# A planned attention kernel: other slots for weight sums, residual loads and one normalisation, and other issuers for six transfers

## The chip, the cores and the metric

The kernel runs on one core of a Trainium2 chip. The metric is the device time of one execution in microseconds (us). A core has five engines with queues of their own: PE (TensorE, matrix products into the accumulator memory PSUM), DVE (VectorE), ACT (ScalarE), POOL (GpSimd) and SP (SyncE, which only issues transfers here). Transfers (DMAs) are issued by SP or by POOL and run beside the engines. An engine works through its own queue in order.

## The reference

For 8 batches of 256 rows with 1024 features, a cross attention with 32 heads of 32 features. Keys and values are the same context tensor:

```
xn  = (x - mean) * rsqrt(var + eps) * gamma + beta
Q   = xn @ Wq.T                 # 32 heads
P   = softmax(mask(Q K^T / sqrt(32)))
out = x + (P V) @ Wout.T
```

All of it is float32.

## The kernel before

**Blocks and slots.** The work is cut into 64 blocks of four heads, n = 0 to 63; batch b owns blocks 8b to 8b+7. The main loop has one slot per block. In slot n PE runs `scores(n + 1)` (16 products, tiles `sc`), some steps of the output projection of an earlier batch (`po_A`, `po_S`), `values(n - 2)` (64 products, tiles `pv`), and products that make queries of a later batch (`pq`, `pq_A`, `pq_S`). In the times below a slot begins with the first score product of block n+1. The scores of a block fill all four PSUM tiles `sc`, so scores of block n+1 can enter a tile only after DVE has taken block n's scores from it.

**Softmax of a block** (`softmax_parts`). For each of four heads j, DVE adds the mask and takes the minimum (L634, `e<-sc,mb`), ACT takes the exponential and its sum (L638), DVE takes the reciprocal (L648, `rden`), and POOL scales the two halves (L654, `e<-e,rden`), or ACT does where the plan's list `scaled` names the pair (block, j) (L652). DVE transposes the result in 32x32 blocks (L660, `pT<-e`), ACT copies half of it aside (L666, `pc<-pT`), and transfers swap the halves between partitions: first `pT<-pT` ("A"), then `pT<-pc` ("B"), both issued at L740. ACT also copies finished queries (`qa`) and values (`at`).

**What else runs beside it.** Batches 1 and 2 are normalised and transposed beside the blocks of batch 0. `ln_stats` takes the statistics on DVE (L339 to L344) and `rstd` on POOL (L347). `ln_norm` applies them, on DVE or POOL in one instruction (L365), or on ACT (L360) after a small instruction on POOL (L357, `shift`). `fold` multiplies a column of Wq by gamma on POOL (L474, 128x1024). From batch 3 on, queries and all output projections use a seven-product scheme in which sums of weight blocks replace an eighth product. `sum_wo` (L290) and `sum_wq` (L504) make these sums, 128x512 each, on the engine that the plan names: P is POOL, V is DVE, A is ACT.

**What sets the order.** A table `PLAN` gives every piece a slot. Inside a slot each engine's order is that of the program text. Entries are relative to the slot in which a batch's query products begin (18 for batch 3, then 26, 34, 42, 50). `wq` and `wo` hold [slot, sum, column, engine]; `foldat` the slot of each fold; `b2`, `b3` and `rel` the slots of loads, statistics, normalisations and transposes of a batch; `st0` and `stg` how many of the 28 projection steps of a batch stand in each of three places of nine slots; `rs0` and `rs` the slots in which four residual tiles `r` are loaded, relative to the batch's first projection slot; `p1late` the batches whose first residual tile is finished later. `keeps` sends finished sums to DRAM.

**Who issues a transfer.** The table `qp`, read in `issue` (L211, L213) and in `swap` (L740, L645), names exceptions to SP: 1 is POOL at once, 2 is POOL at the end of the slot (the call at L1268), and 3 for a swap is POOL just before the next block's first POOL scaling. The swap in question is `sB04`: block 4, first half, back. In a block's tail the order on SP is: swaps A, the loads of the list `between` (keys, rings, residuals, x, weights), swaps B. Residual tiles rotate through four buffers, so a load into one waits until the result that lay there has been sent out; a wait on SP holds everything behind it, swaps B among them. A key load or a residual tile is 256 KB, a value load 512 KB, the two transfers of a swap 128 KB each.

```python
rp = ctx.enter_context(tc.tile_pool(name="rp", bufs=...4))
...
for r in range(2):
    swap(r, False)
for load in between:
    load()
for r in range(2):
    swap(r, True)
```

Of the kernel before, what the change touches and what calls it, by code (L numbers as in the profile page):

```python
# [33 lines left out]


# [1 line left out]
PLAN = {'wq': [[9, 'T1', 0, 'P'], [14, 'T1', 1, 'V'], [15, 'T1', 3, 'V'], [16, 'T3', 2, 'V'], [14, 'T1', 2, 'P'],  # L37
# [13 lines left out]
 'folds': 'PPPPPPPP',  # L51
 'b2': {'loads': [0, 0],
        'stats': [2, 3],
        'norms': [2, 3],
        'trans': [4, 5],
        'moves': [5, 5, 5, 5, 5, 5, 6, 6, 6, 6, 6, 6, 7, 7, 7, 7]},
 'b3': {'loads': [-13, -11],
        'stats': [-10, -9],
        'norms': [-9, -7],
        'trans': [-7, -6],  # L60
        'moves': [-6, -6, -6, -6, -5, -5, -5, -5, -4, -4, -4, -4, -4, -4, -3, -3]},
 'norm2': 'PV',
 'norm3': 'AA',
 'SPLIT': 3,
 'rings': [[-3, -4], [0, 0], [2, 2]],
 'foldat': [-1, 1, 3, 3, 4, 5, 6, 7],
 'st0': [0, 0, 0, 0, 6, 1, 0, 1, 1, 0, 3, 3, 0, 1, 0, 0, 1, 1, 0, 2, 1, 0, 3, 0, 0, 4, 0],
 'stg': [0, 0, 0, 0, 4, 4, 0, 0, 4, 0, 0, 1, 0, 3, 0, 0, 0, 3, 0, 1, 4, 0, 0, 0, 0, 4, 0],
 'rel': {'loads': [-13, -12],
         'stats': [-11, -9],  # L70
         'norms': [-9, -8],
# [1 line left out]
         'moves': [-6, -6, -6, -6, -6, -6, -6, -5, -5, -5, -5, -4, -4, -4, -4, -4]},  # L73
 'woload': [[0, 0, 3], [3, 1, 1], [3, 0, -1], [0, 1, 1], [2, 0, 2], [2, 1, 2]],
 'n11': 'V',
 'p1late': [2, 0],
 'qp': {'sB04': 3,
        'out00': 2,
        'out01': 2,
        'out10': 2,  # L80
        'out11': 2,
# [7 lines left out]
        'r1_01': 2,  # L89
        'mv15': 1,  # L90
        'x1None': 2,
        'mv3_2': 2},
 'vearly': {'30': 'z',
            '44': 'b',
            '54': 'a',
# [5 lines left out]
            '12': 'z',  # L101
            '48': 'a',
            '2': 'z',
            '58': 'b',
            '26': 'b',
            '8': 'a',
            '28': 'z',
            '32': 'b',
            '52': 'b',
            '42': 'b',  # L110
            '38': 'z'},
 'rs': [0, 0, 0, -1],
 'rs0': [0, 1, 2, 3]}

# [15 lines left out]
P = 128  # L130
# [7 lines left out]
def xattn_kernel(  # L138
# [29 lines left out]
    xp = ctx.enter_context(tc.tile_pool(name="xp", bufs=2))  # L168
    rp = ctx.enter_context(tc.tile_pool(name="rp", bufs=PLAN.get('bufs',{}).get('rp',4)))
    lnp = ctx.enter_context(tc.tile_pool(name="lnp", bufs=2))  # L170
    kp = ctx.enter_context(tc.tile_pool(name="kp", bufs=2))
    vp = ctx.enter_context(tc.tile_pool(name="vp", bufs=PLAN.get('bufs',{}).get('vp',2)))
    atp = ctx.enter_context(tc.tile_pool(name="atp", bufs=3))
    ep = ctx.enter_context(tc.tile_pool(name="ep", bufs=PLAN.get('bufs',{}).get('ep',4)))
    ptp = ctx.enter_context(tc.tile_pool(name="ptp", bufs=PLAN.get('bufs',{}).get('ptp',3)))
    asp = ctx.enter_context(tc.tile_pool(name="asp", bufs=PLAN.get('bufs',{}).get('asp',3)))
    up = ctx.enter_context(tc.tile_pool(name="up", bufs=1))
# [23 lines left out]
    xs, ks, vs, rs = {}, {}, {}, {}  # L201
    QP = PLAN.get('qp', {})
    at_end = []
# [1173 lines left out]
```

## Time and profile before

| what | value |
|---|---|
| median of 3 runs | 579.17 us (578.04 to 580.08) |
| the profiled execution's own time | 579.36 us |
| its span, first to last instruction | 577.5 us |
| mean granted TensorE clock | 1.000 |
| instructions | 19967 |
| DVE, ACT, POOL busy | 82%, 74%, 69% of the span |
| DMA: bytes moved, mean rate | 116.93 MB, 202 GB/s |

A row of the timeline reads: start in us from the span's start, duration, engine, line of the kernel, operation, written tile <- read tiles, shape, count; in brackets the idle time of the engine before it and who ended that. A row of the windows reads: stretch, its length, and for each engine the busy time and the number of instructions, then granted clock, share of the DMA engines and GB/s. A row of the groups ends with busy time, mean duration in ns, and idle time before. 1.86 us of the execution's own time lie outside the span.

### The profile page before, as it was taken

To read this page: it belongs to the slowest core of one execution; us is meant where nothing else is said; L and a number is where in the kernel's file an instruction comes from. 1 tells how busy PE (TensorE), PEld (TensorE's weight loads), DVE (VectorE), ACT (ScalarE), POOL (GpSimd) and SP (SyncE) were. 2 spreads that over 40 slices of the span, in tenths; PEclk is the share of its full clock that TensorE was granted. 3 is DMA by queue.
4 is the path that set the end of the run, shared out by engine and by line. 5 is a ranking of instruction groups with operands and counts; after the bars stand their busy time and mean duration, and the time that the engine had idled before them with its cause. 6 is when DMAs were issued, how large, how long until landed. Compare 5 with 4: busy or idle time off the path is not lost.

```text
span 577.5 us, 19967 instructions
## 1 busy us (share of the span) xinstructions
PE 568.4 (98%) x7162; PEld 395.1 (68%) x7162; DVE 470.9 (82%) x1706; ACT 430.0 (74%) x1477; POOL 397.5 (69%) x648
## 2 busy tenths in 40 slices
PE   8999999999999999999999999999999999999997
PEld 8788775667667676678676677667776776755543
DVE  5899799988878889988889888888878687779823
ACT  4697878778588876888588877789868687769820
POOL 2668779888684894866759764596556676358780
PEclk9999999999999999999999999999999999999999
DMA  8767877557687667876698666877577757645751
GB/s 309 261 197 226 233 192 200 155 166 213 192 256 228 182 185 214 249 216 198 185 251 261 192 198 187 251 241 218 163 218 219 206 165 189 183 134 144 191 158 74
DMA packets 45667, 116.93 MB, mean 202 GB/s; under 512 B 9072, under 2 KB 9840, under 8 KB 45568
## 3 DMA queue, kind: packets, MB, share of 16 engines
q1 hardware_dynamic: 42256, 105.61, 63.4%
q0 software_dynamic: 3024, 10.03, 5.3%
q8 instruction: 57, 0.93, 0.7%
q14 instruction: 42, 0.34, 0.2%
q10 hardware_dynamic: 288, 0.01, 0.0%
HBM read 64.23 MB, written 11.53 MB: 131 GB/s over the span
## 4 chain that ended last, share of the span: by engine, by line
PE 64%; DVE 10%; POOL 8%; ACT 6%; DMA 5%; issue 4%; SPq 2%; DVEq 0%; POOLq 0%; ACTq 0%
PE po_S L868 13%; PE pq_A L555 12%; PE po_A L868 9%; PE sc L594 8%; PE pv L778 7%; POOL e L654 6%; PE pq_S L555 5%; PE pq L453 4%; DVE e L634 3%; DMA pT<-pT 3%; ACT e L638 3%; DVE pT L660 3%; PE po_end L935 2%; ACT e L652 1%; SPq L211 1%
## 5 line engine op out<-in xcount | busy, mean ns | idle before, releaser
L654 POOL TENSOR_SCALAR e<-e,rden 128x256 f32<-128x256 f32 x458 | 212.4, 481 | 133.9 <-DVE rden L648 127.2
L638 ACT ACTIVATE e<-e,mn 128x256 f32<-128x256 f32 x512 | 254.0, 501 | 50.1 <-DVE mn L634 50.0
L660 DVE STREAM_TRANSPOSE pT<-e 128x512 f32<-128x512 f32 x256 | 180.5, 707 | 55.2 <-POOL e L654 38.0
L634 DVE CUSTOM_DVE_ANT_0 e<-sc,mb 128x256 f32<-128x256 f32 x512 | 185.1, 415 | 17.8 <-PE sc L594 17.8
L666 ACT COPY pc<-pT 128x512 f32<-128x512 f32 x128 | 79.0, 617 | 56.9 <-DVE pT L660 37.6
L638 ACT ACTIVATION_READ_ACCUMULATOR e<-e,mn 128x1 f32 x512 | 97.9, 191 | 0.0
L453 PE MATMUL pq<-xnT,wq 128*128 128x256 f32 (+1 forms) x368 | 84.2, 382 | 1.7 <-POOL wq L474 0.9
L453 PEld LDWEIGHTS pq<-xnT,wq 128*128 128x128 f32 x368 | 68.7, 190 | 16.8 <-issue 5.0
L594 PE MATMUL sc<-k,qa 32*128 32x256 f32 x1024 | 76.2, 401 | 0.2
L778 PE MATMUL pv<-pT,v 64*32 64x128 f32 x4096 | 74.1, 274 | 0.4 <-PE sc L594 0.4
L868 PE MATMUL po_S<-wo,at 128*128 128x512 f32 x152 | 73.1, 607 | 0.7 <-DVE r L910 0.7
L594 PEld LDWEIGHTS sc<-k,qa 32*128 32x128 f32 x1024 | 47.6, 184 | 37.7 <-issue 16.8
L778 PEld LDWEIGHTS pv<-pT,v 64*32 64x32 f32 x4096 | 57.0, 105 | 23.4 <-issue 14.9
L868 PE MATMUL po_A<-wo,at 128*128 128x512 f32 x128 | 58.5, 602 | 0.6 <-DVE qa L571 0.4
L868 PE MATMUL po_S<-wo,s 128*128 128x512 f32 x104 | 47.9, 597 | 0.0
L555 PEld LDWEIGHTS pq_A<-xnT,wq 128*128 128x128 f32 x352 | 40.6, 192 | 4.9 <-issue 2.5
L868 PEld LDWEIGHTS po_S<-wo,at 128*128 128x128 f32 x152 | 26.3, 190 | 25.2 <-issue 23.9
L634 DVE DVE_READ_ACCUMULATOR2_ANT mn<- 128x1 f32 x512 | 42.1, 82 | 0.0
L555 PE MATMUL pq_A<-xnT,wq 128*128 128x128 f32 x352 | 41.6, 276 | 0.4 <-DVE wq L504 0.4
L868 PEld LDWEIGHTS po_A<-wo,at 128*128 128x128 f32 x128 | 23.3, 190 | 27.2 <-issue 25.1
L648 DVE RECIPROCAL rden<-den 128x2 f32<-128x2 f32 x256 | 37.3, 146 | 2.2 <-ACT e L638 1.5
L791 ACT COPY at<-pv 128x128 f32<-128x128 f32 x128 | 26.2, 253 | 8.7 <-PE pv L778 8.7
(109 smaller groups left out, 654.2 us busy)
## 6 DMA issues: line engine op xcount, KB each, us to landing
v<-in_kv_dram SPq DMA_DIRECT2D x32, 512.0 KB, 5.2
pT<-pT SPq DMA_DIRECT2D x128, 128.0 KB, 3.1
pT<-pc SPq DMA_DIRECT2D x127, 128.0 KB, 3.9
k<-in_kv_dram SPq DMA_DIRECT2D x32, 256.0 KB, 4.5
ring<-kept_T SPq DMA_DIRECT2D x15, 512.0 KB, 5.4
r<-in_x_dram SPq DMA_DIRECT2D x27, 256.0 KB, 5.4
xnT<-xe SPq DMA_DIRECT2D x89, 64.0 KB, 2.5
x<-in_x_dram SPq DMA_DIRECT2D x11, 512.0 KB, 4.6
```

Source lines behind the costliest of these rows:

```text
L453: nc.tensor.matmul(pqs[n], wq[:, o, c, :], xnTs[b](c), start=(c == 0), stop=(c == NC - 1),)
L555: nc.tensor.matmul(pqs[b][:, o, :], w[:, c], x_[:, c], start=begins and o + c == 0, stop=c == NK - 1, skip_group_check=True,)
L594: nc.tensor.matmul(scs[n][j][:, s, :], qa[r, n % NQ, ts(s, P)], ks[n - n % 2][r, n % 2, :], start=True, stop=True,)
L634: nc.vector.tensor_tensor_reduce(out=e[:, s, :], in0=pss[j][:, s, :], in1=mbs[n // NQ], scale=1.0, scalar=NO_SCORE, op0=ALU.add, op1=ALU.m ...
L638: nc.scalar.activation(e[:, s, :], e[:, s, :], AF.Exp, bias=mn[:, s : s + 1], scale=-1.0, accum_out=den[:, s : s + 1],)
L648: nc.vector.reciprocal(rden, dens[j])
L654: engine.tensor_scalar(es[j][:, s, :], es[j][:, s, :], rden[:, s : s + 1], 1.0, ALU.mult, ALU.mult,)
L660: nc.vector.transpose(pT[:, :, :, j, :, :].rearrange("p a i s k -> p (a i) s k"), es[j].rearrange("p s (b t) -> p b s t", t=K),)
L666: nc.scalar.copy(pc[:, :, ts(j, 2)], pT[:, 1, :, ts(j, 2)])
L778: nc.tensor.matmul(pvs[n][r][j * HD : (j + 1) * HD], vs[n - n % 2][ts(r, 2 * K), n % 2, i, ts(j, HD)], pT[ts(r, 2 * K), :, i, j, :, :], st ...
L791: nc.scalar.copy(ats[b, k][:, c, :, ts(r, 2), :], pv.rearrange("p a s k -> p s a k"))
L868: nc.tensor.matmul(po, operand(b, name)[:, c], wo[:, which, c], start=begins and c == 0, stop=c == NK - 1, skip_group_check=not begins,)
```

## The change

Only the table `PLAN` changes; no function does.

- `qp`: the entry for swap `sB04` goes, so SP issues this swap like all others. Three come in: the key loads of blocks 28, 36, 44 and 52 (`k%4`) and a copy of weight sums to DRAM (`keptT31`) are issued by POOL at once, the value load of block 56 by POOL at the slot's end.
- `norm2`: the second half of batch 2 is normalised by ACT instead of DVE (slot 3).
- `wq`: the sums T1 column 3 (slot 15) and T3 column 3 (slot 18) go from DVE to POOL, T4 column 3 (slot 22) from POOL to DVE. The other entries of `wq`, and all of `wo`, keep slot and engine and stand in another order in the list.
- `foldat`: the fold of column 1 goes from slot 1 to slot 0.
- `b3`: the first x load of batch 3 is planned for slot 4 instead of 5, its first normalisation for slot 10 instead of 9.
- `scaled`: one pair more, block 51, j = 1, from POOL to ACT.
- `st0`, `stg`: projection steps of batch 0 in other places of slots 9 to 15; for batches 2 to 5 one step goes from the ninth slot to the eighth, and one changes place within the second.
- `rs0`, `rs`: residual tiles in other slots. For batches 1 to 6, two tiles are loaded in the first projection slot and two in the next, instead of one in the slot before and three in the first.
- `p1late`: batch 3 instead of batch 2 finishes its first residual tile late. `vearly`: the value loads of blocks 58 and 52 stand elsewhere among the loads of their slot.

```diff
- 'wq': ... [15, 'T1', 3, 'V'] ... [18, 'T3', 3, 'V'] ... [22, 'T4', 3, 'P']
+ 'wq': ... [15, 'T1', 3, 'P'] ... [18, 'T3', 3, 'P'] ... [22, 'T4', 3, 'V']
+ 'scaled': ... [51, 1, 'A']
- 'b3': {'loads': [-13, -11], ... 'norms': [-9, -7],
+ 'b3': {'loads': [-14, -11], ... 'norms': [-8, -7],
- 'norm2': 'PV',
+ 'norm2': 'PA',
- 'foldat': [-1, 1, 3, 3, 4, 5, 6, 7],
- 'st0': [0, 0, 0, 0, 6, 1, 0, 1, 1, 0, 3, 3, 0, 1, 0, 0, 1, 1, 0, 2, 1, 0, 3, 0, 0, 4, 0],
- 'stg': [0, 0, 0, 0, 4, 4, 0, 0, 4, 0, 0, 1, 0, 3, 0, 0, 0, 3, 0, 1, 4, 0, 0, 0, 0, 4, 0],
+ 'foldat': [-1, 0, 3, 3, 4, 5, 6, 7],
+ 'st0': [0, 0, 0, 0, 6, 2, 0, 0, 1, 0, 3, 2, 0, 2, 0, 0, 0, 2, 0, 2, 2, 0, 2, 0, 0, 4, 0],
+ 'stg': [0, 0, 0, 0, 5, 3, 0, 0, 4, 0, 0, 1, 0, 3, 0, 0, 0, 3, 0, 1, 4, 0, 0, 1, 0, 3, 0],
- 'p1late': [2, 0],
- 'qp': {'sB04': 3, ...
+ 'p1late': [0, 3],
+ 'qp': {... 'k%4': 1, 'v56': 2, 'keptT31': 1},
- 'vearly': {... '58': 'b', ... '52': 'b', ...
+ 'vearly': {... '58': 'a', ... '52': 'z', ...
- 'rs': [0, 0, 0, -1],
- 'rs0': [0, 1, 2, 3]}
+ 'rs': [0, 1, 1, 0],
+ 'rs0': [0, 0, 2, 3]}
```

More of the change, by code (lines that the diff above doesn't have):

```diff
@@ L36 @@
 import math
-PLAN = {'wq': [[9, 'T1', 0, 'P'], [14, 'T1', 1, 'V'], [15, 'T1', 3, 'V'], [16, 'T3', 2, 'V'], [14, 'T1', 2, 'P'],
[2 rows of a table removed]
+PLAN = {'wq': [[9, 'T1', 0, 'P'], [14, 'T1', 1, 'V'], [15, 'T1', 3, 'P'], [14, 'T1', 2, 'P'], [16, 'T3', 2, 'V'],
[2 rows of a table added]
         [20, 'T2', 3, 'P']],
[2 rows of a table removed]
[2 rows of a table added]
         [7, 4, 0, 'P'], [12, 6, 3, 'P'], [10, 6, 0, 'P'], [13, 3, 0, 'V']],
@@ L56 @@
         'moves': [5, 5, 5, 5, 5, 5, 6, 6, 6, 6, 6, 6, 7, 7, 7, 7]},
- 'b3': {'loads': [-13, -11],
+ 'b3': {'loads': [-14, -11],
         'stats': [-10, -9],
-        'norms': [-9, -7],
+        'norms': [-8, -7],
         'trans': [-7, -6],
         'moves': [-6, -6, -6, -6, -5, -5, -5, -5, -4, -4, -4, -4, -4, -4, -3, -3]},
- 'norm2': 'PV',
+ 'norm2': 'PA',
  'norm3': 'AA',
@@ L75 @@
  'n11': 'V',
- 'p1late': [2, 0],
- 'qp': {'sB04': 3,
-        'out00': 2,
+ 'p1late': [0, 3],
+ 'qp': {'out00': 2,
         'out01': 2,
@@ L91 @@
         'x1None': 2,
-        'mv3_2': 2},
+        'mv3_2': 2,
+        'k%4': 1,
+        'v56': 2,
+        'keptT31': 1},
  'vearly': {'30': 'z',
@@ L103 @@
             '2': 'z',
-            '58': 'b',
+            '58': 'a',
             '26': 'b',
@@ L108 @@
             '32': 'b',
-            '52': 'b',
+            '52': 'z',
             '42': 'b',
             '38': 'z'},
- 'rs': [0, 0, 0, -1],
- 'rs0': [0, 1, 2, 3]}
+ 'rs': [0, 1, 1, 0],
+ 'rs0': [0, 0, 2, 3]}
 from contextlib import ExitStack
```

12 rows, old and new, of the table PLAN are left out of this document.

## The prediction

> **What bounds the kernel now.** I began with the busy table of the page, then had the timeline of PE for the start of each slot, then the windows by slot, and then the timelines of single engines where a slot is too long.
>
> ```profile
> PE 568.4 (98%) x7162; PEld 395.1 (68%) x7162; DVE 470.9 (82%) x1706; ACT 430.0 (74%) x1477; POOL 397.5 (69%) x648
> ```
>
> PE is busy nearly always, so the time is PE's work plus PE's stalls, and the stalls hide in slots that are longer than a twin with the same products. Columns of the windows: stretch, length, then busy time (instructions) of PE, PEld, DVE, ACT, POOL, clock, DMA share, GB/s.
>
> ```profile
> 50.62:58.16 7.54, 7.54 (x106) 6.09 (x105) 6.82 (x24) 3.78 (x14) 6.92 (x6) 1.00 0.61 190
> 58.16:66.07 7.91, 7.58 (x105) 6.08 (x104) 5.55 (x18) 5.74 (x21) 5.53 (x9) 1.00 0.90 242
> 66.07:74.79 8.72, 8.66 (x106) 6.64 (x105) 7.51 (x33) 8.06 (x29) 7.42 (x9) 1.00 0.67 194
> 74.79:83.33 8.54, 8.04 (x105) 6.35 (x105) 8.01 (x24) 5.66 (x21) 5.95 (x10) 1.00 0.92 226
> 83.33:92.90 9.57, 8.66 (x105) 6.44 (x104) 8.51 (x36) 8.43 (x33) 9.10 (x15) 1.00 0.81 207
> 180.91:190.51 9.60, 9.60 (x121) 6.69 (x120) 8.77 (x29) 7.80 (x26) 5.91 (x12) 1.00 0.89 283
> 207.73:216.23 8.50, 8.50 (x119) 6.24 (x118) 7.97 (x29) 5.51 (x20) 8.38 (x14) 1.00 0.61 155
> 216.23:226.36 10.13, 9.04 (x119) 6.23 (x118) 9.37 (x28) 6.24 (x23) 6.44 (x11) 1.00 0.89 241
> 243.24:253.16 9.92, 9.53 (x121) 6.75 (x120) 8.86 (x30) 8.94 (x27) 8.04 (x15) 1.00 0.72 229
> 311.71:321.08 9.37, 9.37 (x122) 6.62 (x121) 8.39 (x30) 8.43 (x27) 8.74 (x16) 1.00 0.57 171
> ```
>
> Slots 4 to 8 (first five rows) do equal work. Against slot 4's 7.54 the next four lose 0.37, 1.18, 1.00 and 2.03, together 4.58 us. Slot 23 loses 10.13 - 8.50 = 1.63 against slot 22. Slots 19 and 26 lose 0.23 and 0.55 against slot 34 (last row). So about 7 us are to be had in these slots; nearly all others run at PE's pace, and there a saving on another engine is worth nothing.
>
> **The change, part by part.**
>
> *Slots 3 to 9: the normalisation and the swap.* Two engines lose time here, DVE and POOL.
>
> ```profile
> 50.77 0.70 DVE L660 STREAM_TRANSPOSE pT<-e 128x512 f32<-128x512 f32 x1
> 52.16 2.38 DVE L365 TENSOR_SCALAR x<-x,mv,rstd 128x1024 f32<-128x1024 f32 x1 [0.69 <-POOL rstd L347]
> 54.45 0.41 DVE L634 CUSTOM_DVE_ANT_0 e<-sc,mb 128x256 f32<-128x256 f32 x1
> 61.37 0.71 DVE L660 STREAM_TRANSPOSE pT<-e 128x512 f32<-128x512 f32 x1 [2.14 <-POOL e L654]
> 63.73 0.39 DVE L634 CUSTOM_DVE_ANT_0 e<-sc,mb 128x256 f32<-128x256 f32 x1
> 51.55 0.57 POOL L347 TENSOR_TENSOR rstd<-ve,mhalf 128x1 f32<-128x1 f32 x1
> 52.09 4.20 POOL L474 TENSOR_TENSOR wq<-wq,gs 128x1024 f32<-128x1024 f32 x2
> 56.59 1.28 POOL L290 TENSOR_TENSOR wo<-wo 128x512 f32<-128x512 f32 x1 [0.31 <-DMA wo<-in_woT_dram]
> 59.60 0.74 POOL L645 DMA_DIRECT2D pT<-pc  x1 [1.73 <-DMA pT<-pT]
> 60.40 1.84 POOL L654 TENSOR_SCALAR e<-e,rden 128x256 f32<-128x256 f32 x4
> 54.97 0.51 ACT L638 ACTIVATE e<-e,mn 128x256 f32<-128x256 f32 x1 [3.76 <-DVE mn L634]
> L360 ACT ACTIVATE x<-x,shift,rstd 128x1024 f32<-128x1024 f32 x10 | 12.4, 1240 | 0.5
> 33.03 3.67 POOL L654 TENSOR_SCALAR e<-e,rden 128x256 f32<-128x256 f32 x8 [2.66 <-DVE rden L648]
> ```
>
> DVE is done with block 4 at 51.47 but waits 0.69 and then spends 2.38 on the normalisation while POOL folds, so block 5 begins at 54.45. Without it DVE can begin when the scores are there, whose slot starts at 50.62; 51.8 is my estimate. The work goes to ACT, which idles for 3.76 until 54.97: POOL's `rstd` ends at 52.12, the one-column `shift` takes no longer than `rstd` itself (0.57), ACT's part 1.24, so ACT's first exponential of block 5 starts by 53.9, at least 1.0 earlier. Cover: this idle stretch; without it the price is 1.24.
>
> That gain alone would stop at POOL. POOL's sum ends at 56.59 + 1.28 = 57.87; then it waits 1.73 for swap A, issues swap `sB04` in 0.74, and only at 60.40 scales block 5. With the swap on SP it can start at 57.87, its first sum of exponentials being ready by then: 2.53 earlier. SP takes one issue more, of about 0.5, between transfers that wait for swap A anyway. DVE's transpose at 61.37 waited for exactly this scaling; the third one then meets ACT's scaling and queue, so of 2.53 I keep 2.3 for block 6's start (63.73 to about 61.4). Ends: 0, if ACT or a transfer holds block 5 just as long, and 2.53.
>
> What is PE's share? PE waits in slot 6 for block 6's score tiles, at the end of slot 8 for a fold:
>
> ```profile
> 66.07 2.32 PE L594 MATMUL sc<-k,qa 32*128 32x256 f32 x16
> 89.25 3.72 PE L453 MATMUL pq<-xnT,wq 128*128 128x256 f32 x16 [0.86 <-POOL wq L474]
> ```
>
> With softmax 2.3 earlier, slot 6 begins at 65.7 with the tiles free; slots 5, 6 and 7 then lose about 0, 0 and 0.2 instead of 0.37, 1.18 and 1.00. Then late is softmax again: ACT is busy for 8.06 in slot 6, DVE for 8.01 in slot 7, POOL for 9.10 in slot 8, all more than PE's 7.54, so slot 8's stalls, the fold among them, move earlier but stay. PE wins **2.35** (2.55 less 0.2). The fold moved to slot 0 (4.20 / 2 = 2.1 at most) fits into the 2.66 that POOL idles ahead of block 2 (row of 33.03) and is worth 0; without that gap it would cost its own length.
>
> The Trainium skill, page "ScalarE: Activation LUTs", section "Rules for kernel authors", sends multiplies and adds to VectorE, not ScalarE, which speaks against `norm2`. By that rule the edit would cost the difference of the two engines; the row of 2.38 shows the opposite for this place. The page "SBUF — State Buffer", section "Who interferes with whom", gives a reason (DVE in a two-port mode and POOL shut each other out for a whole instruction), and the trace agrees here.
>
> *Weight sums.* DVE's sum T1 at slot 15 goes to POOL, as does T3 at slot 18; T4 at slot 22 comes to DVE.
>
> ```profile
> 156.85 0.68 DVE L504 TENSOR_TENSOR ring<-wq 128x512 f32<-128x512 f32 x1
> 160.24 1.29 PE L594 MATMUL sc<-k,qa 32*128 32x256 f32 x16
> 216.02 1.28 POOL L844 TENSOR_TENSOR at<-at 128x512 f32<-128x512 f32 x1
> 216.35 2.34 DVE L584 TENSOR_SCALAR mb<-mk 128x256 f32<-128x256 uint8 x1
> 217.25 1.28 POOL L504 TENSOR_TENSOR wq<-wq 128x512 f32<-128x512 f32 x1
> 218.61 1.28 DVE L504 TENSOR_TENSOR wq<-wq 128x512 f32<-128x512 f32 x2
> 219.94 3.84 PE L555 MATMUL pq_A<-xnT,wq 128*128 128x128 f32 x32 [0.42 <-DVE wq L504]
> 224.45 1.98 PE L868 MATMUL po_S<-wo,at 128*128 128x512 f32 x4 [0.67 <-DVE r L910]
> ```
>
> At slot 17's start PE's scores take 1.29 and slip behind DVE; 0.6 less DVE work just before them gives 0.2 to 0.35, of which I take **0.3**. Slot 19's 0.23 is a wait for DVE too, and the T3 sum just ahead goes: **0.2**. POOL's added sums (1.28 each) fill idle time before its next block. Slot 22: the mask bias on DVE is held until POOL's two sums end (217.25 + 1.28 = 218.53) and is over 0.16 later. With the second gone it is free at 217.30; then come 0.16 and three sums of 0.64: 219.4 instead of 219.9, so DVE begins block 24 between 0.4 and 0.5 earlier. PE's first stall (0.42) goes, its second (0.67) waits for a DVE addition at the end of the same chain and grows; the net is the chain's **0.4**. Were the mask bias slow for another reason, the third sum would cost 0.64.
>
> *Residual tiles, POOL's issues, steps.* On SP three residual loads in the first projection slot wait for a buffer:
>
> ```profile
> 239.59 5.68 SPq L211 DMA_DIRECT2D r<-in_x_dram  x3
> 364.22 1.15 SPq L740 DMA_DIRECT2D pT<-pc  x2
> 371.48 1.16 PE L778 MATMUL pv<-pT,v 64*32 64x128 f32 x64
> L1268 POOL DMA_DIRECT2D x<-in_x_dram x3 | 1.7, 571 | 0.0
> ```
>
> Two of them move a slot on, when the buffers are free, so swaps B come some 4 us earlier. This is worth 0 to PE: even the tightest swap (second half issued at about 364.8) leaves 6.6 us until its values run at 371.48. The four keys cost POOL 0.57 each ahead of a sum, with POOL waiting for DVE soon after; slot 26's stall comes from a value load, and the bytes around it stay about equal, so I count 0 (between +0.9, one more 256 KB ahead of it at the 283 GB/s of slot 19, and -0.55). The projection steps only change places; PE's total is the same, and the slots that get shorter follow longer ones. Pair (51, 1), `keptT31`, `v56`, x of batch 3, `p1late`: 0, all beside slots at PE's pace.
>
> Sum: 2.35 + 0.3 + 0.2 + 0.4 = 3.25. The profiled execution's own 579.36 less 3.25 is 576.1; it stands 0.19 above the median, which gives **575.9**.
>
> **The rivals.**
>
> *The lead grows.* Being ahead, softmax might not fall behind again, and slots 7 to 9 lose nothing. For: POOL then meets fewer collisions. Against: the busy times of 8.01 to 9.10 above, which no lead shortens. It adds 0.2 + 2.03: 573.7.
>
> *The lead is given back.* Block 5 is held by something not shown as a wait now, the sum's weight load (POOL already waits 0.31 for it) or ACT, to within 1 us of today. PE keeps about 1.0 of 2.35 and the other gains shrink to 0.3: 579.17 - 1.3 = 577.9, no measurable change.
>
> *Slower: transfers land too late.* POOL's key loads go out about 4 us sooner, the residuals are no longer held, and both run beside swaps. Swaps land in 3.9 (first row below); a value load in that crowd took 8.4 (second row).
>
> ```profile
> pT<-pc SPq DMA_DIRECT2D x127, 128.0 KB, 3.9
> DMA to landing us min/median/max: 8.4/8.4/8.4
> ```
>
> PE waits from a landing of 6.6 on. At 8.4 each of the four slots would lose 1.8, and with 0.9 for the late value load, 8.1 come against 3.25: 584.0. It turns the sign from 7.4 us of landing (3.25 / 4 + 6.6). Against it: the bytes are the same. The Trainium skill, page "DMA: Bandwidth & Descriptors", section "Issuing engines are not separate DMA queues", says that another issuer saves only issue time, as all share 16 DMA engines; by that rule the key loads bring no gain, and I count none.
>
> **How the numbers follow.** Forecast 0.56, lead grows 0.15, given back 0.16, slower 0.13. 0.3% is 1.7 us, about what a measurement of this kernel can tell from no change. Faster: 0.56 + 0.15 = 0.71, same 0.16, slower 0.13. The range must leave out no more than 0.2: it runs from 573.2 (lead grows, and 0.5 of slot 26) to 579.1 (given back, with 0.9 for the late value load and none of the 0.3), and leaves the slower case out. The forecast's own bounds, 2.53 and 0 on its largest term, lie inside.
>
> **What would show it.** After the change slots 5, 6 and 7 last 7.5 to 7.8, slot 8 still over 9; block 5's first exponential on ACT comes before 54 and POOL's scaling of it before 58.5; no POOL row L645; the mask bias of slot 22 below 1.5; slot 23 near 9.7; residual loads on SP without a wait of 3 us. I am wrong if slot 6 or 7 is still over 8.3, or if values (L778) begin to wait for swaps after slot 24.

## The result, and the profile after

The changed kernel takes **575.20 us** (median of 6 executions, 574.62 to 575.86), the kernel before 579.08 us (6 executions, 578.04 to 580.08): a ratio of 0.9934, with a 95% interval of 0.9921 to 0.9947. That is 3.9 us, or 0.7%, faster; the forecast was 575.9. Its profiled execution took 575.16 us, with a span of 573.4.

To read the single traces one must know that executions of the kernel before fall into two groups: of 61 that ran beside the experiments, 33 took 578.0 to 579.4 us and 28 took 579.9 to 583.4, none in between, while the changed kernel's twelve all took 574.3 to 576.0.

The busy table of the page after, as it answers to the first line shown of before:

```profile
PE 565.7 (99%) x7162; PEld 393.4 (69%) x7162; DVE 466.9 (81%) x1704; ACT 431.5 (75%) x1480; POOL 398.9 (70%) x653
```

The windows of slots 5 to 8, then of slots 19, 23 and 26 (stretch, length, then busy time and instructions of PE, PEld, DVE, ACT, POOL; granted clock, share of the DMA engines, GB/s):

```profile
58.33:65.87 7.54, 7.54 (x106) 6.09 (x105) 6.90 (x25) 6.95 (x24) 6.65 (x9) 1.00 0.90 273
65.87:73.41 7.54, 7.54 (x106) 6.09 (x105) 6.31 (x26) 6.89 (x25) 6.23 (x10) 1.00 0.89 247
73.41:80.95 7.54, 7.54 (x106) 6.09 (x105) 7.29 (x24) 4.67 (x17) 4.80 (x8) 1.00 0.67 185
80.95:90.04 9.09, 8.29 (x105) 6.32 (x104) 8.03 (x33) 7.96 (x31) 8.94 (x15) 1.00 0.82 201
177.97:187.44 9.47, 9.47 (x121) 6.69 (x120) 8.50 (x30) 8.10 (x28) 7.60 (x14) 1.00 0.92 283
213.14:222.62 9.48, 8.77 (x119) 6.31 (x118) 8.72 (x29) 6.23 (x23) 5.18 (x10) 1.00 0.93 263
239.50:248.87 9.37, 9.37 (x122) 6.62 (x121) 8.40 (x30) 8.40 (x27) 8.72 (x16) 1.00 0.75 203
```

Slots 5, 6 and 7 run at PE's pace (busy time equals length). Together with slot 8 they lose 1.55 us where they lost 4.58. Slot 23 is 0.65 shorter, slot 26 0.56, slots 17 and 19 0.14 and 0.13. Where steps of the projection moved, single slots change by up to 0.93, and the slots beside them change the other way: slots 9 to 15 together grow by 0.06, and each of four later pairs by about 0.08. Slots 0 to 4 last what they did, to 0.01.

The timeline of DVE, ACT and POOL around block 5 in the kernel after, engine by engine:

```profile
51.95 0.42 DVE L636 CUSTOM_DVE_ANT_0 e<-sc,mb 128x256 f32<-128x256 f32 x1 [0.33 <-PE sc L596]
60.89 0.39 DVE L636 CUSTOM_DVE_ANT_0 e<-sc,mb 128x256 f32<-128x256 f32 x1
52.67 1.24 ACT L362 ACTIVATE x<-x,shift,rstd 128x1024 f32<-128x1024 f32 x1 [1.29 <-POOL shift L359]
53.82 0.49 ACT L640 ACTIVATE e<-e,mn 128x256 f32<-128x256 f32 x1
52.59 3.75 POOL L476 TENSOR_TENSOR wq<-wq,gs 128x1024 f32<-128x1024 f32 x2
56.30 1.27 POOL L292 TENSOR_TENSOR wo<-wo 128x512 f32<-128x512 f32 x1
57.56 1.84 POOL L656 TENSOR_SCALAR e<-e,rden 128x256 f32<-128x256 f32 x4
```

DVE starts block 5 at 51.95, straight after PE's scores, instead of 54.45. ACT's normalisation (1.24) lies in ACT's idle stretch. POOL goes from its sum to the scaling (57.56 instead of 60.40) without an issue between. Block 6 (second row) starts at 60.89 instead of 63.73. This is the chain of the prediction, down to the estimate of 51.8.

The timeline of slot 23's start: DVE, POOL's one sum, and PE's remaining stall:

```profile
213.25 1.10 DVE L586 TENSOR_SCALAR mb<-mk 128x256 f32<-128x256 uint8 x1
214.27 1.88 DVE L506 TENSOR_TENSOR wq<-wq 128x512 f32<-128x512 f32 x3
216.08 0.41 DVE L636 CUSTOM_DVE_ANT_0 e<-sc,mb 128x256 f32<-128x256 f32 x1
212.91 1.28 POOL L846 TENSOR_TENSOR at<-at 128x512 f32<-128x512 f32 x1
220.71 1.98 PE L870 MATMUL po_S<-wo,at 128*128 128x512 f32 x4 [0.71 <-DVE r L912]
```

The mask bias takes 1.10 instead of 2.34: only one POOL sum lies beside it, and it ends 0.16 behind that sum (214.35 and 214.19), as it ended 0.16 behind POOL's second sum before. The experiment below tests this. Three sums take 1.88, and block 24 starts 2.94 after the slot's beginning (216.08 - 213.14).

### The profile page after: what moved, and what is told of

It reads as the page before. It is cut to its first block, busy times and chain, and to the rows that moved or that the text cites. A ratio compares the mean times of both kernels' runs of the same rounds, so it can differ in the third digit from the quotient of the medians.

```text
span 573.4 us, 19969 instructions
## 1 busy us (share of the span) xinstructions
PE 565.7 (99%) x7162; PEld 393.4 (69%) x7162; DVE 466.9 (81%) x1704; ACT 431.5 (75%) x1480; POOL 398.9 (70%) x653
## 4 chain that ended last, share of the span: by engine, by line
PE 63%; POOL 12%; DVE 10%; ACT 5%; issue 4%; DMA 3%; SPq 1%; DVEq 0%; POOLq 0%
PE po_S L870 13%; PE pq_A L557 12%; PE po_A L870 8%; PE sc L596 8%; POOL e L656 8%; PE pv L780 7%; PE pq_S L557 5%; PE pq L455 5%; DVE e L636 4%; ACT e L640 3%; DVE pT L662 3%; PE po_end L937 2%; DMA pT<-pT 2%; POOL wo L292 1%; DMA wq<-in_wq_dram 1%
## 5 line engine op out<-in xcount | busy, mean ns | idle before, releaser
L656 POOL TENSOR_SCALAR e<-e,rden 128x256 f32<-128x256 f32 x456 | 210.2, 476 | 129.7 <-DVE rden L650 123.1
L596 PE MATMUL sc<-k,qa 32*128 32x256 f32 x1024 | 74.1, 401 | 0.1
L596 PEld LDWEIGHTS sc<-k,qa 32*128 32x128 f32 x1024 | 46.4, 184 | 39.2 <-issue 20.6
```

The source lines that it names most:

```text
L596: nc.tensor.matmul(scs[n][j][:, s, :], qa[r, n % NQ, ts(s, P)], ks[n - n % 2][r, n % 2, :], start=True, stop=True,)
L656: engine.tensor_scalar(es[j][:, s, :], es[j][:, s, :], rden[:, s : s + 1], 1.0, ALU.mult, ALU.mult,)
```

## The experiments

All are measured against the kernel before on the same chip.

| kernel | median us (lowest to highest, executions) | ratio, 95% interval |
|---|---|---|
| norm alone | 578.48 (576.73 to 582.23, 12) | 0.9986 (0.9966 to 1.0007) |
| swap alone | 577.37 (575.97 to 579.73, 12) | 0.9970 (0.9953 to 0.9988) |
| norm and swap | 577.58 (575.36 to 580.09, 12) | 0.9963 (0.9943 to 0.9983) |
| norm, swap, new residual slots | 576.55 (575.08 to 579.27, 12) | 0.9949 (0.9930 to 0.9968) |
| changed, T4 sum on POOL | 575.28 (574.77 to 576.27, 6) | 0.9928 (0.9906 to 0.9950) |
| changed, again | 575.02 (574.28 to 576.01, 6) | 0.9917 (0.9890 to 0.9944) |
| changed, old residual slots | 576.43 (574.58 to 577.32, 8) | 0.9943 (0.9921 to 0.9966) |
| changed, keys on SP | 574.88 (574.52 to 579.12, 8) | 0.9924 (0.9899 to 0.9950) |
| changed, T1 and T3 sums on DVE | 575.31 (574.62 to 576.05, 6) | 0.9919 (0.9900 to 0.9938) |
| changed, one POOL sum later | 574.55 (574.33 to 577.74, 6) | 0.9919 (0.9893 to 0.9944) |

### Who held blocks 5 and 6: DVE, POOL, or both

Theory: DVE's normalisation and POOL's issue hold them one behind the other. Rivals: one of the two alone.

```diff
- 'norm2': 'PV',          # first kernel, and third
+ 'norm2': 'PA',
- 'qp': {'sB04': 3, ...   # second kernel, and third
+ 'qp': {...
```

> The kernel before with one edit: ACT instead of DVE normalises the second half of batch 2. Theory (two engines lose time in turn): DVE begins block 5 at about 52, 2.4 us earlier than its 54.45, but GpSimd still waits for swap A of block 4, issues the swap back, and only then scales block 5. That swap comes only as early as its copies, so block 6 on DVE begins about 1.2 us earlier than 63.73; slots 5 to 8 together lose about 1.2 us less, and the time is about 577.9. Rival A (the normalisation alone held the blocks): block 6 begins over 2.5 us earlier, 576.1. Rival B (GpSimd alone held them): block 6 where it was, 579.1.

> The kernel before with one edit: SP instead of GpSimd issues the swap of block 4, first half, back. Theory: DVE still begins block 5 at about 54.45, after its normalisation, but GpSimd scales block 5 from about 58 instead of 60.40. DVE's transposes still stand behind its own late start, so block 6 begins about 1.5 us earlier than 63.73; slots 5 to 8 lose about 1.5 us less: 577.6. Rival A (GpSimd's issue alone held the blocks): block 6 over 2.5 us earlier, 576.1. Rival B (DVE alone held them): 579.1.

> The kernel before with both edits, the normalisation on ACT and the swap on SP. Theory: these two are all that shortens slots 5 to 8; block 6 on DVE begins at about 60.9 as in the changed kernel, slots 5 to 8 lose 3.0 us less, and the time is 576.1. Rival (the fold moved to slot 0 and the earlier load of x belong to it as well): block 6 begins later than 61.5, and the time is 577 or more.

Norm alone, DVE's start of block 6 and POOL ahead of it:

```profile
62.79 0.39 DVE L634 CUSTOM_DVE_ANT_0 e<-sc,mb 128x256 f32<-128x256 f32 x1
58.66 0.74 POOL L645 DMA_DIRECT2D pT<-pc  x1 [0.85 <-PE pq L453]
59.45 1.85 POOL L654 TENSOR_SCALAR e<-e,rden 128x256 f32<-128x256 f32 x4
```

Swap alone, DVE's normalisation still ahead of block 5, and block 6:

```profile
52.38 2.38 DVE L364 TENSOR_SCALAR x<-x,mv,rstd 128x1024 f32<-128x1024 f32 x1 [0.69 <-POOL rstd L346]
54.68 0.41 DVE L633 CUSTOM_DVE_ANT_0 e<-sc,mb 128x256 f32<-128x256 f32 x1
62.26 0.38 DVE L633 CUSTOM_DVE_ANT_0 e<-sc,mb 128x256 f32<-128x256 f32 x1
```

Both edits, POOL's sum ahead of block 5, and block 6:

```profile
56.90 1.28 POOL L289 TENSOR_TENSOR wo<-wo 128x512 f32<-128x512 f32 x1 [0.44 <-DMA wo<-in_woT_dram]
61.50 0.39 DVE L633 CUSTOM_DVE_ANT_0 e<-sc,mb 128x256 f32<-128x256 f32 x1
```

In each trace slot 0 starts a little earlier or later; with that taken out, block 6 starts this much earlier than in the kernel before, and slots 5 to 8 are this much shorter together:

| trace | block 6 earlier, us | slots 5 to 8 shorter, us |
|---|---|---|
| before, a second trace | -0.01 | -0.01 |
| norm alone | 1.30 | 1.31 |
| swap alone | 1.70 | 1.69 |
| norm and swap | 2.49 | 2.52 |
| norm, swap, new residual slots | 2.73 | 2.74 |
| changed, first and second trace | 3.02, 1.86 | 3.03, 1.88 |
| changed, T4 on POOL | 1.82 | 1.83 |
| changed, old residual slots, two traces | 2.86, 2.56 | 2.88, 2.58 |
| changed, keys on SP | 2.65 | 2.66 |
| changed, one POOL sum later | 3.03 | 3.05 |
| changed, T1 and T3 on DVE | 2.85 | 1.66 |

The theory's 1.2, 1.5 and 3.0 came out as 1.30, 1.70 and 2.49; the 0.5 missing in the third trace is mostly POOL's wait of 0.44 for a weight load (below). The rivals fall: neither edit alone gives 2.5, and with both block 6 begins at 61.24 on the clock of the kernel before, where the rival needed over 61.5. What block 6 wins on DVE, PE wins in slots 5 to 8, to 0.03 us in all rows but the last. The medians show it less sharply, since these kernels spread as the kernel before does: norm alone can't be told from no change, and norm and swap has the rival's 577.6 as its median, though its shortest executions (575.4) lie below the theory's 576.1 and four of its twelve ran with the lower clock of the last section. So the mechanism is shown in the slots of the traces, and the times of the two edits alone show less than it.

### The new neighbour: a weight load

> The changed kernel once more, unedited, as the yardstick for the three beside it and as a second trace. Expected 575.2 us again, with no run over 576.5; slots 23 and 26 at 9.5 and 9.4 us again. Slots 7 and 8 may be longer by up to 0.7 and 0.5 us where the weight load of GpSimd's sum ahead of block 5 lands later (its wait was 0 in one trace and 1.15 us in that with T4 on GpSimd).

The second trace of the changed kernel, POOL ahead of block 5, and PE at slot 6:

```profile
57.45 1.27 POOL L292 TENSOR_TENSOR wo<-wo 128x512 f32<-128x512 f32 x1 [1.12 <-DMA wo<-in_woT_dram]
58.70 1.84 POOL L656 TENSOR_SCALAR e<-e,rden 128x256 f32<-128x256 f32 x4
68.14 1.25 PE L780 MATMUL pv<-pT,v 64*32 64x128 f32 x64 [1.14 <-DMA v<-in_kv_dram]
```

The same program loses 1.14 us of its lead in this execution (58.70 - 57.56, with equal starts), because POOL's sum waits 1.12 for its weights; block 6 follows (1.86 instead of 3.02 earlier), and PE with it. The longer slot is slot 6 (8.85), not slots 7 and 8 as expected. PE's wait for the values in slot 6 costs nothing more here: slots 5 to 8 together still win what block 6 won. The time was still 575.02 in the median.

A candidate for a better version moves that sum behind the blocks:

```diff
- 'wo': [... [3, 5, 2, 'P'], ...
+ 'wo': [... [6, 5, 2, 'P'], ...
```

> The changed kernel with one more edit: GpSimd's output-weight sum that stands ahead of block 5's scaling (T3 column 2, slot 3) moves to slot 6, where GpSimd idles for 2.7 us ahead of block 8. Theory (what is left of the loss in slots 5 to 8 is GpSimd's queue ahead of block 5: the sum's 1.27 us and its wait for the weight load, 0 to 1.15 us): GpSimd scales block 5 from about 56.3, block 6 begins on DVE at about 59.6, slots 5 to 7 last 7.54, slot 8 about 8.0 instead of 9.09, and the time is about 573.9. Rival (ACT or DVE is the bound there by now): slot 8 stays over 8.8 and the time is about 575.

POOL's timeline in that kernel:

```profile
52.38 3.75 POOL L476 TENSOR_TENSOR wq<-wq,gs 128x1024 f32<-128x1024 f32 x2
56.11 1.84 POOL L656 TENSOR_SCALAR e<-e,rden 128x256 f32<-128x256 f32 x4
59.23 0.93 POOL L656 TENSOR_SCALAR e<-e,rden 128x256 f32<-128x256 f32 x2 [1.28 <-DVE rden L650]
```

POOL scales at 56.11, as expected, but then waits 1.28 for DVE's reciprocals: block 6 starts 3.03 us earlier than before, no more than the changed kernel's best. So the rival holds for the lead: at 3.0 us DVE and ACT are the bound. Its sign in the slots does not: slot 8 goes to 8.15, but slot 6 takes the difference (8.47, a wait for the swap). The median of 574.55 can't be told from the changed kernel's 575.02 and 575.20.

### The sums

```diff
- [22, 'T4', 3, 'V']                      # one kernel
+ [22, 'T4', 3, 'P']
- [15, 'T1', 3, 'P'] ... [18, 'T3', 3, 'P']   # another
+ [15, 'T1', 3, 'V'] ... [18, 'T3', 3, 'V']
```

> The changed kernel with one edit undone: the sum T4 column 3 of slot 22 on GpSimd again. Theory (the mask bias on DVE is held until both of GpSimd's sums have ended): the mask bias of slot 22 takes about 2.3 us again, slot 23 goes from 9.48 back to about 10.1 us, and the time rises by 0.6 to about 575.8. Rival (the steps of the projection or the residual loads shortened slot 23): it stays near 9.5 us and the time near 575.2.

With T4 on POOL again, DVE and then POOL at the start of slot 23:

```profile
213.72 2.34 DVE L586 TENSOR_SCALAR mb<-mk 128x256 f32<-128x256 uint8 x1
215.98 1.28 DVE L506 TENSOR_TENSOR wq<-wq 128x512 f32<-128x512 f32 x2
217.18 0.41 DVE L636 CUSTOM_DVE_ANT_0 e<-sc,mb 128x256 f32<-128x256 f32 x1
213.38 1.28 POOL L846 TENSOR_TENSOR at<-at 128x512 f32<-128x512 f32 x1
214.61 1.29 POOL L506 TENSOR_TENSOR wq<-wq 128x512 f32<-128x512 f32 x1
```

The mask bias is back at 2.34 and ends 0.16 behind POOL's second sum (216.06 and 215.90); slot 23 lasts 10.11 instead of 9.48. The rival falls: the projection steps and residual slots are as changed here, and the slot is long again. The sum's engine is worth 0.63 us in the slot. The median (575.28) does not resolve it.

> The changed kernel with two edits undone: the sums T1 column 3 (slot 15) and T3 column 3 (slot 18) on DVE again. Theory as forecast: 0.5 us more, slot 17 at 12.3 and slot 19 at 9.6. Theory after the traces so far: slot 17 12.07 to 12.16 instead of 12.02, slot 19 unchanged, no more than 0.15 us in the time, 575.1. Rival (DVE's time just ahead of slot 17 makes the last transposing transfers late, so that these sums belong to what removed the spread): a highest run over 577 and a median near 576.

Slot 17 stays at 12.02 and slot 19 at 9.37 with both sums on DVE, and the time is 575.31. The forecast's theory and the rival miss. The second theory is right that next to nothing is lost, and wrong about slot 17. These two edits are worth nothing that can be seen, and the 0.1 of slot 17 comes from another part of the change, not found. This trace has the one row of the table in which a lead was lost, at PE in slot 6:

```profile
69.60 1.25 PE L780 MATMUL pv<-pT,v 64*32 64x128 f32 x64 [2.76 <-DMA v<-in_kv_dram]
```

The value load was issued at 59.86; from then to 69.60 the DMA engines were 99% busy. A wait of 2.76 is more than slot 8 can give back, so 1.2 us are lost (slot 9 gives back 0.26 of them).

### Residual tiles, keys, and the spread

```diff
- 'rs': [0, 1, 1, 0],  'rs0': [0, 0, 2, 3]    # changed kernel, old residual slots
+ 'rs': [0, 0, 0, -1], 'rs0': [0, 1, 2, 3]
- 'k%4': 1,                                   # changed kernel, keys on SP
```

> The changed kernel with one edit undone: the residual tiles loaded in their old slots (for batches 1 to 6 one in the slot before the first projection slot, three in that slot). Theory (the old places put a residual load ahead of the last two transposing transfers of x on SP's queue near 160 us, and GpSimd's sums of x wait for these; PE then waits at slot 18 in some executions, 2.5 us in the trace of the norm alone, and its granted clock drops behind the wait): the runs spread again, the highest over 577, the median 576 to 576.5. Rival (the residual loads cost nothing, as forecast; other edits removed the spread): 575.2 and no run over 576.5.

> The kernel before with three edits: normalisation on ACT, swap on SP, and the residual tiles in their new slots. The first two alone gave 577.6 with runs from 575.4 to 580.1. Theory (residual slots remove the wait at slot 18): no run over 577, median 575.5 to 576. Rival (the new order of sums, steps or key loads removes it): median 577 to 578 and a highest run near 580, as without the third edit.

> The changed kernel with one edit undone: the key loads of blocks 28, 36, 44 and 52 issued by SP again. Theory (all transfers share the DMA engines, and SP has time there): no difference, 575.2 within 0.3, slot 26 still 9.37. Rival (the 0.56 us that slot 26 won came from these loads' issue on GpSimd): slot 26 back at about 9.9 and 575.8 or more.

> The changed kernel with the residual tiles in their old slots, a second look: its eight runs went from 574.6 to 577.3, and the one with a trace was the fastest. Theory (GpSimd's sums of x wait at slot 18 for the last two transposing transfers): in a run near 576.5 or above slot 18 lasts 9.5 us or more instead of 8.51, behind a wait of these sums for a transfer. Rival (the time goes elsewhere): slot 18 at 8.51 in such a run, and the loss in other slots.

Keys: no difference in the median, and slot 26 is at 9.37 with either issuer. Residual tiles: with the old slots six of eight executions took 576.2 to 577.3, more than any of the changed kernel's twelve, which points to about 1.4 us (576.43 - 575.02), though the two intervals overlap. But both traces fell on executions shorter than these six (574.58 and 575.31), and in both slot 18 lasts 8.51, so where the six lose their time was not seen. Added to norm and swap, the new residual slots gave a median of 576.55, between theory and rival, and left three of twelve executions above 577, against the theory's none. So the residual slots are not the whole of it; which edits took the spread away stays open.

The second of the two traces does lose 0.55 us, in slot 17 (12.57 instead of 12.02). DVE, POOL and PE there:

```profile
161.41 1.76 DVE L506 TENSOR_TENSOR wq<-wq 128x512 f32<-128x512 f32 x1
161.33 1.28 POOL L545 TENSOR_TENSOR sx<-xnT 128x512 f32<-128x512 f32 x1
167.20 2.84 PE L870 MATMUL po_A<-wo,at 128*128 128x512 f32 x6 [0.29 <-ACT p L878]
```

POOL's sum of x (`sx`) begins beside DVE's weight sum, which takes 1.76 instead of 0.65, so DVE begins block 18 1.1 us later in the slot. The first trace of the same program has no such meeting, so this belongs to the execution.

How time is lost at slot 18 is clearer. In the norm-alone trace (580.5 us of span) POOL and PE near slot 18:

```profile
169.40 1.26 POOL L543 TENSOR_TENSOR sx<-xnT 128x512 f32<-128x512 f32 x1 [5.87 <-issue]
176.50 1.25 POOL L543 TENSOR_TENSOR xnT<-xnT,sx 128x512 f32<-128x512 f32 x1
177.77 5.44 PE L555 MATMUL pq_S<-sx,ring 128*128 128x128 f32 x32 [2.54 <-POOL xnT L543]
```

POOL idles 5.87 us ahead of its sums of x: the two transposing transfers that they need were issued by SP from 163.19 on, and the second took 5.0 us to land. All that POOL has queued behind these sums is late too. Slots 18 and 19 together, over 17.88, against the time from the sums' start to slot 18's start:

| trace | sums start ahead of slot 18 | slots 18 and 19 lose |
|---|---|---|
| old residual slots, two traces | 6.95, 8.64 | 0, 0 (the second loses 0.55 in slot 17) |
| changed, second trace | 6.92 | 0 |
| before, first trace | 6.53 | 0.23 |
| norm, swap, new residual slots | 6.14 | 0.59 |
| changed, first trace | 6.04 | 0.10 |
| before, second trace | 5.31 | 1.45 |
| swap alone | 4.35 | 2.40 |
| norm alone | 2.21 | 4.73 |

In the other five traces the sums start 6.75 to 7.70 ahead and nothing is lost. In five of the six traces that lose, lead and loss add up to 6.7 to 6.9 us: below that lead each further us costs about one. The first trace of the changed kernel is the exception. In the norm-alone trace 1.7 of the loss are a lower clock (last section). This is correlation over fourteen traces; no edit moved these sums alone.

> The kernel before once more, for a second trace. Theory (its stalls of 0.56 us at slot 26 and 0.2 at slots 19 and 21 came with one execution's transfers, since traces of kernels that leave those slots as they were show them at 9.37, 9.37 and 8.51): at least two of these three are gone here, while slots 6, 7, 8 and 23 are again at about 8.7, 8.5, 9.6 and 10.1. Rival (they belong to the kernel before): all three are there again.

The second trace of the kernel before, of an execution of 580.58 us, POOL and PE:

```profile
166.79 1.27 POOL L543 TENSOR_TENSOR sx<-xnT 128x512 f32<-128x512 f32 x1 [2.66 <-issue]
189.51 1.98 PE L868 MATMUL po_S<-wo,at 128*128 128x512 f32 x4 [0.77 <-DVE r L906]
432.27 0.63 PE L778 MATMUL pv<-pT,v 64*32 64x128 f32 x22 [0.41 <-issue]
```

Slots 6, 7, 8 and 23 are at 8.73, 8.55, 9.58 and 10.05, as in the first trace: these stalls belong to the program. Slot 26 is at 9.37, so its 0.56 us belonged to one execution; slot 21 (8.70) came again, and slot 19 was worse (10.40), so one of three was gone where two were expected. Slots 18 and 19 lose 1.45, slot 48 0.78 by a late swap. These 2.2 us are about the distance of the two groups (medians 578.57 and 580.74).

## Why the prediction came out right, step by step

**Slots 5 to 8** (forecast 2.35). Mechanism right, by the two edits alone and together. In the compared pair the term is 3.03, but that is the most of any trace with slots 3 to 9 as changed: over these seven it is 2.36 on average (1.66 to 3.03). So 2.35 agrees with this average and falls 0.7 short of the pair. The forecast's 2.3 for block 6 left 0.2 to a queue; what takes it is the weight load, between 0 and 1.15 us in these traces, which the prediction had only as a doubt in "the lead is given back". That slot 8's stalls stay (9.09) was right. How much of the 2.38 us of DVE's normalisation is its meeting with POOL's fold the working did not say: the same instruction takes 0.80 elsewhere on DVE (last section).

**Slot 22 and 23** (0.4). The cause was right, the term too small: 0.65. The working had DVE at block 24 between 0.4 and 0.5 earlier, and PE's second stall growing by what the first one lost. Block 24 comes 0.64 earlier (2.94 after the slot's beginning instead of 219.81 - 216.23 = 3.58; three sums take 1.88, not 1.92, and follow at once), and the second stall stays at 0.71 beside 0.67 before.

**Slots 17 and 19** (0.3 and 0.2). This step failed. "0.6 less DVE work just before them" moved nothing: the slots are the same with the sums on DVE. A slot that is 0.2 us longer in one trace was taken for a stall of the program: slot 19 lasts 9.37 in nine of the fourteen traces, whichever engine has the sums.

**Slot 26** (0, between +0.9 and -0.55). 0 was right for the program: the slot lasts 9.37 in every other trace, with either residual slots and either issuer of the keys, and in the second trace of before. The compared pair shows 0.56 because in one execution the value load, issued at 236.30, landed only at 244.68.

**Residual tiles** (0). Not settled: about 1.4 us by the medians, not seen in a trace. The working looked at the latest swaps and at one execution.

**Steps of the projection** (0). Slightly wrong: slots 31 and 32, 39 and 40, 47 and 48, 55 and 56 are each 0.08 longer as a pair, 0.33 us together.

**The fold in slot 0 and the other parts** (0). Right: slots 0 to 4, and those from 49 to 54, last the same.

**Terms that were missing.** The sum of the right terms, 2.36 + 0.65 + 0.1 (slot 17) + 0.1 (slot 41) - 0.33 = 2.9, is less than the 3.9 of the medians. The two traces of the kernel before point to where the rest lies, in stalls that only some of its executions have: 0.8 us in its first trace (slots 19 and 26), 2.2 in its second. Which edit rid the changed kernel of them is open. The forecast was drawn from one trace and couldn't see them; it came out near the result partly by luck, because its terms of 0.5 for the sums stood where other gains were.

**The rivals.** Each left a trace. The lead is partly given back, by the weight load. Transfers do land late, at a place that was not named: PE waits in slot 6 for values or a swap in four of the eight traces of the changed kernel and its variants, 0.8 to 2.8 us, and loses by it in one. The lead does not grow: at 3.0 us DVE and ACT hold it. Of the signs named for the profile all came out in the compared trace except slot 23 (9.48, below the 9.7). In the second trace of the same program three more did not: POOL scales block 5 at 58.70, not before 58.5, slot 8 lasts 8.94, not over 9, and slot 6 lasts 8.85, over the 8.3 that was named as a sign of being wrong. That sign took a late landing for a wrong mechanism.

## What to carry to other kernels

Where PE is busy throughout, follow the block that starts late: here what softmax won at one block, PE had won to 0.03 us by the end of the next three slots in all traces but one. Before a stall of a few tenths becomes a term of a forecast, look whether a second trace of the same kernel has it. And two holders of one block are found by removing each alone: one gave 1.30, the other 1.70, of the 3.0 that both can give.

## What the hardware did that was not expected

**The clock after a wait.** Norm alone, PE in three stretches around the end of its wait of 2.54 us, which began at 175.23; then, with T1 and T3 on DVE, two stretches around its wait of 2.76 us, which began at 66.84:

```profile
174.64:178.05 3.41, 0.87 (x4) 1.00 0.69 224
178.05:181.46 3.41, 3.41 (x18) 0.50 0.34 77
181.46:184.88 3.42, 3.42 (x24) 1.00 0.75 225
64.69:68.11 3.42, 2.15 (x21) 1.00 0.95 226
68.11:71.52 3.41, 1.92 (x67) 1.00 0.87 296
```

The column behind PE's busy time is the granted clock. In the first trace it halves for 3.41 us, and 32 products take 5.44 instead of 3.73: the wait of 2.5 us cost 4.7 with its consequences. The wait of 2.76 us in the second trace was followed by a clock of 1.00. The Trainium skill, page "TensorE: Matmul & The Clock Gate", section "What's actually happening", says that the clock is halved after at least one idle window of about 3.4 us, is full again after a busy one, and that the windows run free of the program. The half clock and its length agree with the trace; the wait that set it off was shorter than such a window.

The traces suggest why one wait did it and the other did not. The granted clock is recorded at 1.00 for 170.67 us ahead of the half clock in the first trace and for 566.61 us in the second: 50 and 166 times 3.413. Counted in such steps, the stretches above are the windows. The shorter wait lies wholly in one, in which PE was busy for 0.87 of 3.41 us; the longer is divided between two, in which PE was busy for 2.15 and 1.92. This is one wait of each kind, and no run moved a wait against the windows.

One such stretch brings the mean granted clock of an execution to 0.997 (half of 3.41 us in 575). Four of the twelve executions of norm and swap have a mean clock of 0.997 (577.7 to 580.1 us), two each of swap alone and of norm, swap and new residual slots, one of norm alone, the one long execution with the keys on SP (579.12), and, at 0.996, that with one POOL sum later (577.74). None of the changed kernel's twelve has it, and only one of the 61 of the kernel before, so the two groups are something else.

**POOL beside DVE.** The kernel before has the same normalisation on DVE in other places, without a fold of POOL beside it:

```profile
6.55 0.80 DVE L365 TENSOR_SCALAR x<-x,mv,rstd 128x1024 f32<-128x1024 f32 x1
```

It takes 0.80 there and 2.38 beside POOL's folds; on ACT it takes 1.24. So ACT is not the faster engine for it: of the 2.38 us that the edit takes from DVE, 1.58 go with the meeting. POOL's two folds take 4.20 beside DVE's normalisation and 3.75 beside ACT's. The mask bias on DVE takes 2.34 beside two POOL sums and 1.10 beside one, ending each time 0.16 behind POOL's last sum, and DVE's weight sum took 1.76 instead of 0.65 beside POOL's sum of x.
